# A state-space scan and window attention in one kernel: output products summed by accumulating DMAs from GpSimd's queue

## The chip, the cores and the metric

The kernel runs on one core of one Trainium2 chip. A core has four compute engines with in-order instruction queues of their own: TensorE (PE in the profile; its weight loads are PEld), VectorE (DVE), ScalarE (ACT) and GpSimd (POOL). SyncE (SP) issues DMA transfers, which 16 DMA engines carry out. Engines wait for each other by semaphores. The metric is the device time of one execution in microseconds (us). Before the change it is 7846.2 us, the median of three runs (7838.49 to 7853.48).

## What is computed

The reference applies two layers to x of shape 8 x 192 x 64 x 64 in float32.

Layer 0 widens 192 channels to 384 by a 1x1 product, applies a 3x3 depthwise convolution, and then scans the image in four directions d (rows, columns, and both flipped). Each direction and channel has gates made from a 16-channel proxy. The part that matters here, per direction:

```
hn  = l * x + gl * h_up + gm * h + gr * h_dn      # 8 steps, chunks of 8
out = out * Us + xs * Ds                          # two products for each direction
y   = einsum('bdchw,d->bchw', out_y, w_m)         # the sum over the four directions
y   = grn(layernorm2d(y)); return conv1x1(y, W_out)
```

Layer 1 is window attention with 6 heads on 8x8 windows (layer norm, normalised q and k, only scores at or above the 16th largest kept, softmax, projection) and a feed-forward part with GELU, each with a residual.

## The kernel before

The kernel is one program over 8 images. For each image `front` makes the convolved input and writes it to DRAM in two layouts, `scan` makes the sum y, and `window_row` does layer 1 for 8 rows of 8 windows. Image b is scanned while the windows of image b-1 and the front of image b+1 run. A tile is 128 channels by 512 positions. In `scan`, each of 8 steps t has 12 tiles, four directions times three blocks of 128 channels (`ct`), in the order of `TILES`: directions 0, 2, 1, 3. So an image has 96 tiles, and the program 768.

A tile's work (`tile_of` and `rest`, lines 685 to 816): TensorE makes the gates (L681), ScalarE takes their absolute values (L738, L760), VectorE multiplies gates by the state (L745, L747), GpSimd and VectorE add up the gates' sum and the products (L769, L777, L784, L788), ScalarE makes a reciprocal by Ln and Exp (L780, L782), and VectorE writes the new state (L810). Tiles go in pairs (`PAIRS`). When the second tile of a pair has its state, `outputs` makes four products on TensorE in four of the six PSUM banks, and `onto_sum` (L834) handles each of the two tiles: VectorE writes `dx` (L836) and `hu` (L841), two products of a PSUM bank with the input and with the state. GpSimd then does the sum over directions in the tile `y3` (128 x 3 x 512, two buffers):

- direction 0: `y3 = hu + dx`, one addition (L848);
- direction 2: `dx = dx + hu` (L850), then `y3 = y3 + dx` (L856);
- directions 1 and 3: the same with L850, then L858, where dx is read with a stride of 64 elements, because these directions hold a tile as columns x rows (`by`), while y3 is kept as rows x columns.

`norm` (L864) takes the finished y3: mean over channels on TensorE (L871), spread back (L883), subtract on VectorE (L894), squares on ScalarE (L899), and so on, then SP writes it to DRAM (L931).

The order of instructions on each engine is not the program order. Every call of `plan` makes a `Step` with an engine, a cost in nanoseconds (hold and latency), and what it reads and writes. `Plan.order` runs a list scheduler over all steps with these costs (`vec`, `act`, `gp`, `mg`, `dma`) and with a model of TensorE's clock (`TICK`, `ENTRY`), repeats it `RUNS` times with ranks taken from the last run, keeps the shortest, and then writes the steps down in that order. Dependencies become semaphore waits. So a change of a cost changes the order on all engines, but no instruction's own time. Tiles in SBUF (`Held`) have a tag and a number of buffers; a step that needs a buffer waits for the last user of an earlier one. In `window_row` the transposed q and k (`qkT`, tag `four`, two tiles of two buffers, L1186) are made by TensorE's transposes (L1192), and the feed-forward's hidden tile `hd` (one buffer, L1455) is read by L1496.

Of the kernel before, what the change touches and what calls it, by code (L numbers as in the profile page):

```python
# [26 lines left out]
ALU = mybir.AluOpType  # L27
# [27 lines left out]
class Held:  # L55
# [11 lines left out]
    def __call__(self):  # L67
        return self.tile
# [9 lines left out]
class Plan:  # L78
# [5 lines left out]


    HOP = 35.0
    TICK, ENTRY = 10240 / 3, 3060.0
    RUNS = 12
    SLACK = 40.0

    def __init__(self):
# [1 line left out]
        self.parts = {}  # L93
        self.rank, self.lane = 0.0, 0

    def __call__(self, engine, cost, fn, r=(), w=()):
        s = Step(engine, fn, cost, self.rank, self.lane, len(self.steps))
        self.steps.append(s)
        deps = set()
        for item in r:  # L100
            for k in self._overlaps(item, self.writers):
                deps.update(self.writers[k])
        for item in w:
            for k in self._overlaps(item, self.writers):
                deps.update(self.writers[k])
            for k in self._overlaps(item, self.readers):
                deps.update(self.readers[k])
        for item in list(r) + list(w):
            h = item[0] if isinstance(item, tuple) else item
            if isinstance(h, Held) and s not in h.users:  # L110
                if not h.users:
                    s.makes.append(h)
                else:
                    deps.add(h.users[0])
                h.users.append(s)
                s.held.append(h)
# [12 lines left out]
        deps.discard(s)  # L129
        s.before = len(deps)  # L130
        for d in deps:
            d.after.append(s)
        return s
# [12 lines left out]
    def order(self):  # L146

        before = [s.before for s in self.steps]
        tiles = {h: h.left for s in self.steps for h in s.held}
        best = None
        for _ in range(self.RUNS):
            for s, k in zip(self.steps, before):
                s.before, s.ready = k, 0.0
            for h, k in tiles.items():
                h.left, h.end, h.next = k, 0.0, None  # L160
            run = self.run()
            if best is None or self.length < best[0]:
                best = self.length, run, [s.start for s in run]
            for s in run:
                needs = [d.start for d in s.after] + [h.next.start for h in s.held if h.next]
                s.rank = min(needs, default=s.end) - (s.end - s.start)
        self.length, run, starts = best
        for s, t in zip(run, starts):
            s.start = t
        return run  # L170
# [118 lines left out]
def tile_ss2d_then_window_attention(ctx: ExitStack, tc: tile.TileContext, a: dict, out: bass.AP):  # L289
# [170 lines left out]
    vec = lambda n: (n / 0.96 + 69, 88)  # L460
    act = lambda n, more=50.0: (n / 1.2 + more, 110)
    gp = lambda n: (n * 2.3 + 52, 42)
    mm = lambda slots, n, share=1.0: (65.0, slots * n * 4.16, share)
    tiled = lambda cycles, share=1.0: (150.0, cycles, share)
    split = (275.0, 6475.0, 1.0)
    turned = lambda n, share=1.0: (60.0, 262.0 * n, share)

    mg = lambda share=1.0: (120.0, 2270.0, share)
    dma = lambda n=1, kb=0: (max(350.0 * n, 5.4 * kb), 2600.0)
    tiny = (150.0, 60.0)  # L470
    log_c = {}
    log_half = blank("log_half", [P, 1], math.log(0.5) / 3)
# [143 lines left out]
    def scan(b, xs, xsT, z, made):  # L616
# [68 lines left out]
        def tile_of(t, d, ct, xp, x0, y3, last):  # L685
# [85 lines left out]
            if last:  # L771
                last()

            def rest():
                if t > 0:
                    rr = Held(spool, [P, 512], "rr", bufs=2)
# [20 lines left out]
                        w=[nb],  # L797
                    )
                    plan("POOL", gp(512), lambda: nc.gpsimd.tensor_mul(one(), one(), rr()), r=[rr], w=[(pr, 0)])  # L799
                    plan(  # L800
                        "DVE",
                        vec(512),
                        lambda: nc.vector.scalar_tensor_tensor(nb(), nb(), 2.0, one(), ALU.subtract, ALU.mult),  # L803
                        r=[(pr, 0)],
                        w=[nb],
                    )
                    plan(
                        "DVE",
# [4 lines left out]
                    )  # L813
                waiting.append((d, ct, xd, xv, h_key))
                if len(waiting) == 2:
                    outputs(waiting, nb if t > 0 else None)

            def outputs(pair, nb):

                banks = [[bank("g") for _ in range(2)] for _ in range(2)]  # L820

                at = PAIRS.index(tuple(p[:2] for p in pair)) * P

                def both():
                    for k in range(2):
                        for m in range(2):
                            project(banks[k][m](), w_g2, 64 * k + RG * m, RG, at, xp())

                plan("PE", mg(), both, r=[xp, nb] if nb else [xp], w=banks[0] + banks[1])
                for (d, ct, xd, xv, h_key), (pd, pu) in zip(pair, banks):  # L830
                    onto_sum(d, ct, xd, xv, h_key, pd, pu)
                pair.clear()

            def onto_sum(d, ct, xd, xv, h_key, pd, pu):  # L834
                dx = Held(spool, [P, 512], "dx")
                plan("DVE", vec(512), lambda: nc.vector.tensor_mul(by(dx(), d), by(pd(), d), xv()), r=[pd, xd], w=[dx])  # L836
                hu = Held(spool, [P, 512], "hu")
                plan(
                    "DVE",
                    vec(512),  # L840
                    lambda: nc.vector.tensor_mul(like(hu(), d), like(pu(), d), state(d, ct)),  # L841
                    r=[pu, h_key],
                    w=[hu],
                )
                yt = lambda: y3()[:, ct, :]
                y_key = y3, ct
                if d == 0:
                    plan("POOL", gp(512), lambda: nc.gpsimd.tensor_add(yt(), hu(), dx()), r=[hu, dx], w=[y_key])  # L848
                    return
                plan("POOL", gp(512), lambda: nc.gpsimd.tensor_add(dx(), dx(), hu()), r=[hu], w=[dx])  # L850

                def onto():
                    y = by(yt(), 0)
                    if d == 2:

                        nc.gpsimd.tensor_add(y, y, by(dx(), 0))  # L856
                    else:
                        nc.gpsimd.tensor_add(y, y, dx().rearrange("p (c i) -> p i c", c=CH))  # L858

                plan("POOL", gp(512) if d == 2 else (1540.0, 40.0), onto, r=[dx], w=[y_key])  # L860

            return rest

        def norm(t, y3):  # L864
# [22 lines left out]
            m4 = Held(spool, [P, P], "m4", tag="xq", bufs=1)  # L887
            plan("PE", tiled(1553.0), lambda: means(pm, y3), r=[y3], w=[pm])
            plan("ACT", act(P), lambda: nc.scalar.copy(m4(), pm()[:, 0:P]), r=[pm], w=[m4])
            plan("PE", tiled(2203.0), lambda: spread(pm, m4), r=[m4], w=[pm])  # L890
            plan(
                "DVE",
                vec(1536),
# [26 lines left out]
                r=[pv],  # L920
                w=[sq],
            )
            plan("PE", tiled(2203.0), lambda: spread(pv, rr), r=[sq], w=[pv])
            plan(
                "DVE",
                vec(1536),
# [85 lines left out]
    def window_row(b, g, z, sc, bb):  # L1012
# [170 lines left out]
        plan("DVE", (2373.0, 90.0), unit, r=[nn], w=[qk])  # L1183
        yield
        plan.lane = 8
        qkT = [Held(lpool, [HALF, 2, GT], "four", bufs=2) for _ in range(2)]  # L1186
        for k in range(4):
            pt = bank()

            def turn(k=k, pt=pt):  # L1190
                for tt in range(NT):
                    nc.tensor.transpose(  # L1192
                        pt()[0:HALF, tt * P : (tt + 1) * P], qk()[:, tt, k * HALF : (k + 1) * HALF], ident
                    )

            plan("PE", turned(4), turn, r=[qk], w=[pt, (qkT[k // 2], "room")])
            plan(
                "ACT",
                act(512),
                lambda k=k, pt=pt: nc.scalar.copy(qkT[k // 2]()[:, k % 2, :], pt()[0:HALF, :]),  # L1200
                r=[pt],
                w=[(qkT[k // 2], k % 2)],
            )
            yield

# [8 lines left out]
        def scores():  # L1214
            for w in range(WS):
                tok = slice(w * 64, w * 64 + 64)
                for r in range(3):
                    rows = slice(32 * r, 32 * r + 32)
                    for j in range(2):
                        nc.tensor.matmul(  # L1220
                            pas[r]()[64 * j : 64 * j + 64, tok],
                            lhsT=qkT[0]()[rows, j, tok],
                            rhs=qkT[1]()[rows, j, tok],
                            start=True,
                            stop=True,
                        )

        plan("PE", tiled(2550.0, 0.6), scores, r=qkT, w=pas + [(at, "room")])
        for r in range(3):
            rng = slice(r * WS, (r + 1) * WS)  # L1230
            plan(
# [114 lines left out]
                                stop=True,  # L1346
                            )

        plan("PE", tiled(2350.0, 0.5), attend, r=[at, v], w=po + [("oT", "room")])
        for w in range(2):  # L1350
            plan(
                "ACT",
# [288 lines left out]
```

## Time and profile before

| what | value |
|---|---|
| median of three runs | 7846.2 us |
| profiled execution, its own time | 7831.69 us |
| its span, first to last instruction | 7829.6 us |
| mean granted TensorE clock | 0.849 |
| GpSimd's additions for the sum: L850, L858, L848, L856 | 738.2 + 593.4 + 252.6 + 250.1 us busy, 1344 instructions |
| VectorE's products for the sum: L841, L836 | 517.8 + 388.7 + 130.2 us busy, 1536 instructions |
| DMA moved | 695.53 MB, mean 89 GB/s |

The profile is that of one execution. Busy time is when an engine works on an instruction; idle time before an instruction is put down to what released it last. Instructions that only issue DMAs are not counted as busy. A stage in which an engine is busy 90% of the time may be bound by it; one in which three engines are all near that needs a look at who waits for whom. In a list of waits a row reads: engine and instruction that waited, the instruction that it waited for, total us, times, longest. In a table of stretches a row reads: the stretch in us, its length, busy us and number of instructions of PE, PEld, DVE, ACT and POOL, the granted clock, the DMA engines' busy share and GB/s.

### The profile page before, as it was taken

To read this page: it belongs to the slowest core of one execution; us is meant where nothing else is said; L and a number is where in the kernel's file an instruction comes from. 1 tells how busy PE (TensorE), PEld (TensorE's weight loads), DVE (VectorE), ACT (ScalarE), POOL (GpSimd) and SP (SyncE) were. 2 spreads that over 40 slices of the span, in tenths; PEclk is the share of its full clock that TensorE was granted. 3 is DMA by queue.
4 is the path that set the end of the run, shared out by engine and by line. 5 is a ranking of instruction groups with operands and counts; after the bars stand their busy time and mean duration, and the time that the engine had idled before them with its cause. 6 is when DMAs were issued, how large, how long until landed. Compare 5 with 4: busy or idle time off the path is not lost.

```text
span 7829.6 us, 144584 instructions
## 1 busy us (share of the span) xinstructions
PE 6807.6 (87%) x51224; PEld 3516.3 (45%) x51224; DVE 6279.8 (80%) x15421; ACT 4911.0 (63%) x9657; POOL 6212.0 (79%) x6302
## 2 busy tenths in 40 slices
PE   5788888888999889889998889988888898788888
PEld 2333344444444444444444444444444444344554
DVE  1377778899788978889889888888899989999443
ACT  1355446775666656766677656767566656666665
POOL 0388878899788978888889878888799989899332
PEclk8788779987898878888898779988878878788998
DMA  7666445312543135322553124431211121111110
GB/s 183 181 170 167 125 123 146 100 50 65 151 115 78 47 112 137 87 69 59 140 141 85 44 85 129 115 80 51 58 48 49 50 61 51 46 47 46 25 25 14
DMA packets 1037929, 695.53 MB, mean 89 GB/s; under 512 B 704116, under 2 KB 860215, under 8 KB 1037207
## 3 DMA queue, kind: packets, MB, share of 16 engines
q1 hardware_dynamic: 1035830, 684.99, 33.0%
q8 instruction: 407, 6.67, 0.4%
q14 instruction: 316, 2.58, 0.1%
q10 hardware_dynamic: 1376, 1.30, 0.1%
HBM read 453.43 MB, written 232.67 MB: 88 GB/s over the span
## 4 chain that ended last, share of the span: by engine, by line
DVE 21%; PE 19%; POOL 15%; ACT 8%; issue 4%; DMA 0%; POOLq 0%; SPq 0%; ACTq 0%; DVEq 0%
PE g L681 6%; PE lp L1496 4%; POOL pr L799 3%; POOL ab L769 2%; POOL pr L784 2%; DVE rest L1249 2%; POOL dx L850 2%; PE lp L1105 2%; POOL pr L788 2%; DVE pr L745 2%; DVE nb L803 1%; DVE pr L747 1%; PE lp L1462 1%; POOL y L858 1%; DVE top L1247 1%
## 5 line engine op out<-in xcount | busy, mean ns | idle before, releaser
L681 PE MATMUL g<-xe,w_g 32*128 32x512 f32 x3648 | 1273.0, 768 | 271.1 <-DVE dx L836 106.9
L681 PE MATMUL g<-xo,w_g 32*128 32x512 f32 x3648 | 1156.1, 728 | 218.5 <-DVE dx L836 123.8
L784 POOL TENSOR_TENSOR pr<-pr 128x512 f32<-128x512 f32 x672 | 878.0, 1307 | 192.7 <-DVE pr L745 137.1
L769 POOL TENSOR_TENSOR ab<-ab 128x512 f32<-128x512 f32 x672 | 873.3, 1300 | 162.6 <-ACT ab L738 157.8
L738 ACT ACTIVATE ab<-g 128x512 f32<-128x512 f32 x1344 | 782.2, 596 | 333.3 <-PE nb L681 145.7
L799 POOL TENSOR_TENSOR pr<-pr,rr 128x512 f32<-128x512 f32 x672 | 869.2, 1294 | 125.7 <-ACT rr L782 106.9
L788 POOL TENSOR_TENSOR pr<-pr 128x512 f32<-128x512 f32 x672 | 865.4, 1289 | 17.2
L850 POOL TENSOR_TENSOR dx<-dx,hu 128x512 f32<-128x512 f32 x576 | 738.2, 1290 | 121.8 <-DVE hu L841 108.2
L780 ACT ACTIVATE rr<-nb,eps 128x512 f32<-128x512 f32 x672 | 461.3, 686 | 566.5 <-DVE nb L777 564.4
L681 PEld LDWEIGHTS g<-xe,w_g 32*128 32x128 f32 x3648 | 447.3, 216 | 811.2 <-DVE dx L836 227.8
L568 PE MATMUL lp<-strip,w_cv 128*32 128x256 f32 x9216 | 682.0, 440 | 142.5 <-DMA strip<-pad 123.5
L681 PEld LDWEIGHTS g<-xo,w_g 32*128 32x128 f32 x3648 | 390.9, 206 | 731.5 <-DVE dx L836 250.2
L1496 PE MATMUL lp<-hd,w_f 128*64 128x256 f32 (+1 forms) x2304 | 585.1, 492 | 33.7 <-ACT hd L1482 23.6
L795 DVE SCALAR_TENSOR_TENSOR nb<-nb,rr 128x512 f32<-128x512 f32 x672 | 464.5, 691 | 186.8 <-ACT rr L782 185.9
L858 POOL TENSOR_TENSOR y<-y,dx 128x512 f32<-128x512 f32 x384 | 593.4, 1554 | 2.2
L803 DVE SCALAR_TENSOR_TENSOR nb<-nb,pr 128x512 f32<-128x512 f32 x672 | 464.4, 691 | 152.0 <-POOL pr L799 149.7
L777 DVE TENSOR_TENSOR nb<-nb,ab 128x512 f32<-128x512 f32 x672 | 464.5, 691 | 110.3 <-POOL ab L769 94.2
L568 PEld LDWEIGHTS lp<-strip,w_cv 128*32 128x32 f32 x9216 | 304.5, 123 | 543.0 <-issue 274.3
L848 POOL TENSOR_TENSOR y<-hu,dx 128x512 f32<-128x512 f32 x192 | 252.6, 1320 | 340.6 <-DVE hu L841 337.9
L841 DVE TENSOR_TENSOR hu<-g,hid 128x512 f32<-128x512 f32 x768 | 517.8, 678 | 4.9 <-PE g L681 4.4
L681 PE MATMUL nb<-xe,w_g 32*128 32x512 f32 x672 | 511.9, 852 | 11.1 <-DVE hid L810 8.8
L760 ACT ACTIVATE nb<-nb 128x512 f32<-128x512 f32 x672 | 398.7, 593 | 183.6 <-DVE pr L745 107.7
(203 smaller groups left out, 16680.0 us busy)
## 6 DMA issues: line engine op xcount, KB each, us to landing
strip<-pad SPq DMA_DIRECT2D x1152, 132.0 KB
xd<-xsT SPq DMA_DIRECT2D x384, 256.0 KB
pad<-xin SPq DMA_DIRECT2D x192, 264.0 KB
xs<-st SPq DMA_DIRECT2D x192, 256.0 KB
xsT<-sn SPq DMA_DIRECT2D x192, 256.0 KB
xd<-xs SPq DMA_DIRECT2D x192, 256.0 KB
x<-xs SPq DMA_DIRECT2D x64, 768.0 KB
z<-y SPq DMA_DIRECT2D x64, 768.0 KB
```

Of the source, the lines that this page charges most:

```text
L568: nc.tensor.matmul(pc()[q * RG : (q + 1) * RG, k * 256 : (k + 1) * 256].rearrange("p (h w) -> p h w", h=4), lhsT=w_cv[:, ct, q, dx, :], rh ...
L681: nc.tensor.matmul(dst, lhsT=w[rows, col : col + P], rhs=xp[rows, :], start=True, stop=True)
L738: lambda r=r: nc.scalar.activation(ab()[:, r, :], g[r](), AF.Abs),
L769: plan("POOL", gp(512), lambda: nc.gpsimd.tensor_add(ab()[:, 0, :], ab()[:, 0, :], ab()[:, 1, :]), w=[ab])
L784: plan("POOL", gp(512), lambda: nc.gpsimd.tensor_add(one(), one(), pr()[:, 1, :]), r=[(pr, 1)], w=[(pr, 0)])
L788: lambda: nc.gpsimd.tensor_add(one(), one(), pr()[:, 2, :]),
L799: plan("POOL", gp(512), lambda: nc.gpsimd.tensor_mul(one(), one(), rr()), r=[rr], w=[(pr, 0)])
L803: lambda: nc.vector.scalar_tensor_tensor(nb(), nb(), 2.0, one(), ALU.subtract, ALU.mult),
L841: lambda: nc.vector.tensor_mul(like(hu(), d), like(pu(), d), state(d, ct)),
L850: plan("POOL", gp(512), lambda: nc.gpsimd.tensor_add(dx(), dx(), hu()), r=[hu], w=[dx])
L858: nc.gpsimd.tensor_add(y, y, dx().rearrange("p (c i) -> p i c", c=CH))
L1496: nc.tensor.matmul(dst[:, at : at + rhs.shape[-1]], lhsT=lhsT, rhs=rhs, **flags)
```

## The change

Each pair of tiles now gets two joint tiles `dxu` of 128 x 2 x 512: one for the two products with the input, one for the two with the state. VectorE writes the products there (L863, L873 in the changed kernel), already in y3's order: in directions 1 and 3 with a stride of 8 elements. For direction 0 the product with the input goes straight into y3. GpSimd's additions are gone; in their place GpSimd's queue issues DMAs that add a joint tile onto y3 in SBUF (`accum_op`): eleven for each step t, 704 in all, 640 of 512 KB and 64 of 256 KB (L883, L893). The tile `qkT` becomes one tile of four blocks that shares the single buffer of `hd`; the DMA descriptors' room in SBUF goes from 512 to 2048 bytes. The planner gets a cost for the new DMA (1000 ns hold, 2500 ns latency), other constants for TensorE's clock and shares, 30 repetitions in place of 12, and ranks that are averaged with those of the run before. The output products of a pair no longer read `nb`; they are ordered behind the steps that made the pair's last state factors (`made_w`).

```diff
-    TICK, ENTRY = 10240 / 3, 3060.0
-    RUNS = 12
+    TICK, ENTRY = 10240 / 3, 3200.0
+    RUNS = 30
...
-    def __call__(self, engine, cost, fn, r=(), w=()):
+    def __call__(self, engine, cost, fn, r=(), w=(), behind=()):
...
-        deps = set()
+        deps = set(behind)
...
-                s.rank = min(needs, default=s.end) - (s.end - s.start)
+                rank = min(needs, default=s.end) - (s.end - s.start)
+                s.rank = (s.rank + rank) / 2 if n else rank
...
-    mm = lambda slots, n, share=1.0: (65.0, slots * n * 4.16, share)
+    mm = lambda slots, n, share=0.96: (65.0, slots * n * 4.16, share)
...
-    mg = lambda share=1.0: (120.0, 2270.0, share)
+    mg = lambda share=0.9: (120.0, 2270.0, share)
...
+    accumulate = (1000.0, 2500.0)
...
-                plan("PE", mg(), both, r=[xp, nb] if nb else [xp], w=banks[0] + banks[1])
-                for (d, ct, xd, xv, h_key), (pd, pu) in zip(pair, banks):
-                    onto_sum(d, ct, xd, xv, h_key, pd, pu)
+                plan("PE", mg(), both, r=[xp], w=banks[0] + banks[1], behind=made_w)
+                onto_sum(pair, banks)
...
-            def onto_sum(d, ct, xd, xv, h_key, pd, pu):
...
-                if d == 0:
-                    plan("POOL", gp(512), lambda: nc.gpsimd.tensor_add(yt(), hu(), dx()), r=[hu, dx], w=[y_key])
-                    return
-                plan("POOL", gp(512), lambda: nc.gpsimd.tensor_add(dx(), dx(), hu()), r=[hu], w=[dx])
...
-                plan("POOL", gp(512) if d == 2 else (1540.0, 40.0), onto, r=[dx], w=[y_key])
+            def onto_sum(pair, banks):
+
+                cts = [p[1] for p in pair]
+                lo, step = min(cts), abs(cts[1] - cts[0])
+                parts = Held(spool, [P, 2, 512], "dxu", bufs=3), Held(spool, [P, 2, 512], "dxu", bufs=3)
+
+                def order_y(ap, d):
+
+                    return like(ap, d) if d % 2 == 0 else ap.rearrange("p (i c) -> p c i", c=CH)
+
+                for m, part in enumerate(parts):
+                    todo = []
+                    for (d, ct, xd, xv, h_key), bank2 in zip(pair, banks):
+                        src = bank2[m]
+                        first = m == 0 and d == 0
...
+                                lambda dst=dst, src=src, xv=xv, d=d: nc.vector.tensor_mul(
+                                    order_y(dst(), d) if d % 2 else by(dst(), d), by(src(), d), xv()
+                                ),
...
+                                lambda dst=dst, src=src, d=d, ct=ct: nc.vector.tensor_mul(
+                                    order_y(dst(), d), like(src(), d), state(d, ct)
+                                ),
...
+                    if len(todo) == 2:
+                        plan(
+                            "POOL",
+                            accumulate,
+                            lambda part=part: nc.gpsimd.dma_start(
+                                y3()[:, lo : lo + step + 1 : step, :], part(), accum_op=ALU.add
+                            ),
+                            r=[part],
+                            w=[(y3, ct) for ct in todo],
+                        )
...
-        qkT = [Held(lpool, [HALF, 2, GT], "four", bufs=2) for _ in range(2)]
+        qkT = Held(lpool, [HALF, 4, GT], "four", bufs=1, tag="hd")
...
-    nc = bacc.Bacc("TRN2", target_bir_lowering=False, num_devices=1, dynamic_dma_scratch_size=512)
+    nc = bacc.Bacc("TRN2", target_bir_lowering=False, num_devices=1, dynamic_dma_scratch_size=2048)
```

More of the change, by code (lines that the diff above doesn't have):

```diff
@@ L155, in order @@
         best = None
-        for _ in range(self.RUNS):
+        for n in range(self.RUNS):
             for s, k in zip(self.steps, before):
@@ L462, in tile_ss2d_then_window_attention @@
     gp = lambda n: (n * 2.3 + 52, 42)
-    mm = lambda slots, n, share=1.0: (65.0, slots * n * 4.16, share)
+    mm = lambda slots, n, share=0.96: (65.0, slots * n * 4.16, share)
     tiled = lambda cycles, share=1.0: (150.0, cycles, share)
-    split = (275.0, 6475.0, 1.0)
+    split = (275.0, 6475.0, 0.95)
     turned = lambda n, share=1.0: (60.0, 262.0 * n, share)
-    mg = lambda share=1.0: (120.0, 2270.0, share)
+    mg = lambda share=0.9: (120.0, 2270.0, share)
     dma = lambda n=1, kb=0: (max(350.0 * n, 5.4 * kb), 2600.0)
+    accumulate = (1000.0, 2500.0)
     tiny = (150.0, 60.0)
@@ L772, in tile_of @@
                 last()
+            made_w = []
             def rest():
@@ L799, in rest @@
                     plan("POOL", gp(512), lambda: nc.gpsimd.tensor_mul(one(), one(), rr()), r=[rr], w=[(pr, 0)])
[L800 to L805, printed above, removed]
+                    made_w.append(
+                        plan(
+                            "DVE",
+                            vec(512),
+                            lambda: nc.vector.scalar_tensor_tensor(nb(), nb(), 2.0, one(), ALU.subtract, ALU.mult),
+                            r=[(pr, 0)],
+                            w=[nb],
+                        )
                     )
@@ L815, in rest, with outputs @@
                 if len(waiting) == 2:
-                    outputs(waiting, nb if t > 0 else None)
-            def outputs(pair, nb):
+                    outputs(waiting, made_w)
+            def outputs(pair, made_w):
                 banks = [[bank("g") for _ in range(2)] for _ in range(2)]
@@ L827, in both @@
                             project(banks[k][m](), w_g2, 64 * k + RG * m, RG, at, xp())
-                plan("PE", mg(), both, r=[xp, nb] if nb else [xp], w=banks[0] + banks[1])
-                for (d, ct, xd, xv, h_key), (pd, pu) in zip(pair, banks):
-                    onto_sum(d, ct, xd, xv, h_key, pd, pu)
+                plan("PE", mg(), both, r=[xp], w=banks[0] + banks[1], behind=made_w)
+                onto_sum(pair, banks)
                 pair.clear()
-            def onto_sum(d, ct, xd, xv, h_key, pd, pu):
[L835 to L846, printed above, removed]
-                if d == 0:
-                    plan("POOL", gp(512), lambda: nc.gpsimd.tensor_add(yt(), hu(), dx()), r=[hu, dx], w=[y_key])
-                    return
[L850 to L858, printed above, removed]
-                plan("POOL", gp(512) if d == 2 else (1540.0, 40.0), onto, r=[dx], w=[y_key])
@@ new lines, in onto_sum @@
+            def onto_sum(pair, banks):
[9 more added lines that the diff above has]
+                        first = m == 0 and d == 0
+                        if first:
+                            dst = lambda ct=ct: y3()[:, ct, :]
+                        else:
+                            dst = lambda part=part, ct=ct: part()[:, int(ct > lo), :]
+                            todo.append(ct)
+                        if m == 0:
+                            plan(
+                                "DVE",
+                                vec(512),
+                                lambda dst=dst, src=src, xv=xv, d=d: nc.vector.tensor_mul(
+                                    order_y(dst(), d) if d % 2 else by(dst(), d), by(src(), d), xv()
+                                ),
+                                r=[src, xd],
+                                w=[(y3, ct) if first else (part, ct)],
+                            )
+                        else:
+                            plan(
+                                "DVE",
+                                vec(512),
+                                lambda dst=dst, src=src, d=d, ct=ct: nc.vector.tensor_mul(
+                                    order_y(dst(), d), like(src(), d), state(d, ct)
+                                ),
+                                r=[src, h_key],
+                                w=[(part, ct)],
+                            )
+                    if len(todo) == 2:
+                        plan(
+                            "POOL",
[5 more added lines that the diff above has]
+                            w=[(y3, ct) for ct in todo],
+                        )
+                    elif todo:
+                        plan(
+                            "POOL",
+                            accumulate,
+                            lambda part=part, ct=todo[0]: nc.gpsimd.dma_start(
+                                y3()[:, ct, :], part()[:, int(ct > lo), :], accum_op=ALU.add
+                            ),
+                            r=[part],
+                            w=[(y3, todo[0])],
+                        )
@@ L889, in norm @@
             plan("ACT", act(P), lambda: nc.scalar.copy(m4(), pm()[:, 0:P]), r=[pm], w=[m4])
-            plan("PE", tiled(2203.0), lambda: spread(pm, m4), r=[m4], w=[pm])
+            plan("PE", tiled(2203.0, 0.93), lambda: spread(pm, m4), r=[m4], w=[pm])
             plan(
@@ L922, in norm @@
             )
-            plan("PE", tiled(2203.0), lambda: spread(pv, rr), r=[sq], w=[pv])
+            plan("PE", tiled(2203.0, 0.93), lambda: spread(pv, rr), r=[sq], w=[pv])
             plan(
@@ L1194, in turn @@
                     )
-            plan("PE", turned(4), turn, r=[qk], w=[pt, (qkT[k // 2], "room")])
+            plan("PE", turned(4), turn, r=[qk], w=[pt, (qkT, "room")])
             plan(
@@ L1199, in window_row @@
                 act(512),
-                lambda k=k, pt=pt: nc.scalar.copy(qkT[k // 2]()[:, k % 2, :], pt()[0:HALF, :]),
+                lambda k=k, pt=pt: nc.scalar.copy(qkT()[:, k, :], pt()[0:HALF, :]),
                 r=[pt],
-                w=[(qkT[k // 2], k % 2)],
+                w=[(qkT, k)],
             )
@@ L1221, in scores @@
                             pas[r]()[64 * j : 64 * j + 64, tok],
-                            lhsT=qkT[0]()[rows, j, tok],
-                            rhs=qkT[1]()[rows, j, tok],
+                            lhsT=qkT()[rows, j, tok],
+                            rhs=qkT()[rows, 2 + j, tok],
                             start=True,
@@ L1226, in scores @@
                         )
-        plan("PE", tiled(2550.0, 0.6), scores, r=qkT, w=pas + [(at, "room")])
+        plan("PE", tiled(2550.0, 0.6), scores, r=[qkT], w=pas + [(at, "room")])
         for r in range(3):
@@ L1347, in attend @@
                             )
-        plan("PE", tiled(2350.0, 0.5), attend, r=[at, v], w=po + [("oT", "room")])
+        plan("PE", tiled(2350.0, 0.65), attend, r=[at, v], w=po + [("oT", "room")])
         for w in range(2):
```

## The prediction

> **What bounds the kernel now.** First the busy shares of the page, then the table of stretches: the start until the first output products (0 to 290 us), the eight scans (290 to 7290), the last image's windows (7290 to 7829), and two stretches without a front stage.
>
> ```profile
> PE 6807.6 (87%) x51224; PEld 3516.3 (45%) x51224; DVE 6279.8 (80%) x15421; ACT 4911.0 (63%) x9657; POOL 6212.0 (79%) x6302
> 0.00:290.00 290.00, 176.33 (x1457) 79.25 (x1458) 28.59 (x69) 60.46 (x85) 2.29 (x8) 0.80 0.73 188
> 290.00:7290.00 7000.00, 6181.81 (x45749) 3154.64 (x45748) 6014.45 (x14175) 4511.16 (x8866) 6056.22 (x5968) 0.85 0.34 90
> 7290.00:7829.00 539.00, 449.45 (x4022) 282.46 (x4018) 236.74 (x1180) 339.41 (x707) 153.49 (x328) 0.90 0.09 20
> 5700.00:6100.00 400.00, 351.19 (x2298) 185.43 (x2295) 371.64 (x922) 275.68 (x551) 369.28 (x376) 0.83 0.18 51
> 6500.00:6900.00 400.00, 329.99 (x2399) 175.41 (x2400) 366.12 (x850) 260.32 (x517) 369.40 (x364) 0.84 0.17 48
> ```
>
> All that the change touches lies in the 7000 us. There PE is busy 88.3%, POOL 86.5%, DVE 85.9%. PE's figure contains its slow clock (0.85): at full clock the same work is about 6182 x 0.85 = 5255 us, 75%. So PE is not the bound; DVE and POOL are, level with each other. Neither is full, because each waits for the other and for PE and ACT. The list of waits shows it, with PE held by DVE, which empties PSUM:
>
> ```profile
> PEld g L681 <- DVE dx L836: 478.0, 343, 8.3
> DVE nb L795 <- ACT rr L782: 185.9, 159, 4.4
> DVE nb L803 <- POOL pr L799: 149.7, 162, 4.2
> POOL pr L784 <- DVE pr L745: 137.1, 86, 5.1
> PE lp L568 <- DMA strip<-pad: 123.5, 41, 8.1
> ```
>
> The price of GpSimd's additions, and of strided access, is in the groups, kept apart by shape:
>
> ```profile
> L850 POOL TENSOR_TENSOR dx<-dx,hu 128x512 f32<-128x512 f32 x576 | 738.2, 1290 | 121.8 <-DVE hu L841 108.2 <-DVE dx L836 11.6 <-ACT ab L738 0.2
> L858 POOL TENSOR_TENSOR y<-y,dx 128x512 f32<-128x512 f32 x384 | 593.4, 1554 | 2.2
> L848 POOL TENSOR_TENSOR y<-hu,dx 128x512 f32<-128x512 f32 x192 | 252.6, 1320 | 340.6 <-DVE hu L841 337.9 <-DVE dx L836 2.1
> L856 POOL TENSOR_TENSOR y<-y,dx 128x512 f32<-128x512 f32 x192 | 250.1, 1306 | 1.6
> L582 ACT ACTIVATE st<-lp,vecs 128x512 f32<-128x512 f32 x192 | 222.9, 1161 | 179.0 <-PE lp L568 158.3 <-DMA xsT<-sn 7.4 <-ACT xin L533 5.3
> L595 ACT ACTIVATE sn<-lp,vecs 128x512 f32<-128x512 f32 x192 | 128.6, 670 | 1.2 <-DMA xsT<-sn 1.2
> ```
>
> L858 differs from L856 only in reading dx with a stride: +248 ns. L582 writes what L595 writes, with a stride of 64 elements: +491 ns, twice the time.
>
> **What the Trainium skill says.** "DMA: Bandwidth & Descriptors", section "SWDGE vs HWDGE vs iDMA": a DMA that accumulates must come from GpSimd, whose cores compute its descriptors, so GpSimd stays occupied for each. The same page, "Rules for kernel authors": an accumulating DMA reads its destination and writes it later, so another one onto the same bytes must wait for the first one's semaphore. No such DMA is in this trace. "SBUF — State Buffer", section "A bandwidth-pool intuition that's wrong (but worth ruling out)", gives lines of 16 bytes and a penalty for each access that crosses into a new one. The ACT and POOL rows above agree with it. "VectorE: DVE Perf Modes", section "Mode 1×", says of VectorE's one-result-per-cycle mode that "fp32, weird strides, PSUM operands" all work, and counts unused port width alone as its cost. No strided VectorE write is in this trace, so nothing here decides between the two pages.
>
> **The change, part by part.**
>
> Removed: the four groups of additions, 738.2 + 593.4 + 252.6 + 250.1 = 1834 us of POOL, all in the 7000 us. POOL's work there falls from 6056 to 4222 us.
>
> Added on POOL: 704 DMA issues. The page on DMA puts GpSimd's start of a DMA at about 1 us (section "Specifications"); SP's issues of xd (L697) in this trace take 0.33 us. I bound the hold at 0.6 to 1.5 us and take 1.0: 704 us, so 4926.
>
> Added as a wait: in the changed order of instructions, 640 of the 704 wait for an earlier DMA of the same sum, and POOL is in order, so the gate additions behind (L769, L784, L788, L799 of before) wait too, and DVE's L777 and L803 for those. Pricing the POOL instructions that stand between two such DMAs by their rows of before, the gap is under 0.65 us in 57 cases and under 3.5 us in 301. Landing: the page's fit ("Anatomy of one DMA — SWDGE (gpsimd) path") is 2.0 + bytes / 436e3 us, 3.2 us for 512 KB; the destination is also read, and SP's transfers use the same 16 engines. As an estimate I take 3.5 us after the issue, between 2.5 and 6. The sum of (landing - gap) over the cases below it is 281 us at 2.5, 561 at 3.5, 1052 at 5, 1404 at 6. So POOL is taken for 4926 + 561 = 5487 us, 78% of 7000; between 4222 + 422 + 281 = 4925 and 4222 + 1056 + 1404 = 6682.
>
> DVE: the count of products is the same, 1536. In directions 1 and 3, 768 of them now write with a stride of 32 bytes. Below: 0. Above: one more cycle for each of 512 elements, 533 ns (ACT's twofold time carried over), 768 x 0.533 = 409 us. In the likeliest case I take 0, since DVE's element takes 1.04 ns against 0.83 of ACT, and keep the other for the range. A second new wait on DVE is for a free `dxu`: three buffers, two for each pair. A pair comes every 7000 / 384 = 18.2 us; one part is held some 1.4 + 1.0 + 3.5 = 6 us, the other 4.5 us longer, about 16 of 3 x 18.2 buffer-us, so waits should be few; at a landing of 6 us it is some 24.
>
> DMA engines: 352 MB more, 808 us of all engines if each byte passes once, 1616 if twice. The share 0.34 becomes 0.46 to 0.57. The cover is the rest; the price, if transfers stretch by a fifth, is about 25 us on PE's 123.5 us for strips and a fifth of SP's landings, which loads ahead.
>
> Edits at nothing: the shared buffer of `qkT` and `hd` makes L1192 wait for both halves of L1496, where before it could run between them. In the scans other PE work covers that; in the last 539 us it would cost at most 8 rows x 3.4 us (the second half's 2.8 + 0.6) = 27 us. The mean over channels on PE now waits for the last landings of a step, and everything behind it on PE too: 64 x 3.5 = 224 us if it came straight behind, nothing if the order leaves the planned 2.5 us; 64 us for one us too little. It is counted within the utilisation below. `behind` instead of `nb` drops a wait on DVE's last read at most. The new order as such has no price from a row; it is in the spread.
>
> The sum for the likeliest case: DVE remains, with 6014 us to do. Where POOL and DVE were level it was busy 85.9%; the best stretch shows 92.9% (371.64 of 400). With POOL at 78% and new DMA waits I take the middle, 89.4%: 6014 / 0.894 = 6727 us in place of 7000, a gain of 273. The span becomes 7829.6 - 273 = 7557. The profiled execution's own time is 2.1 us above its span and the median 14.5 us above that: 7574 us. PE would then need 5255 / 6727 = 78% of full-clock time, which needs a clock near 0.88 at 89% busy; before 0.85.
>
> **Rivals.**
>
> Better: DVE runs at 92.9% throughout, since nothing level with it is left: 6014 / 0.929 = 6474, -526, about 7320 us. For it: the best stretches have POOL at 92% too, so DVE without it could go there. Against: those lack the front stage, and ACT's and PE's waits remain.
>
> Slower, by VectorE's strided writes: 409 us more work, 6423 / 0.894 = 7185, +185, about 8032 us. Break-even is (7000 x 0.894 - 6014) / 768 = 0.32 us more for each write. For it: ACT's and POOL's rows. Against: POOL's 248 ns would still leave a gain.
>
> POOL's blocked queue takes the place of the additions: hold and stalls together reach 1834 us at a hold of 1.0 when the landing is 5.2 us. At 5.5 us (1228 us of stalls) POOL has 6154 us, +98; at its present 86.5% that is +113, about 7960. For it: 344 of 640 gaps are under 5 us. Against: part of these stalls falls into time in which POOL waits anyway.
>
> PE is what holds: it is busy 88.3%, and its clock sinks when it is fed badly; if its rate can't rise, the time stays at about 7840. Against: 0.90 with 90% busy occurs elsewhere (the last stretch has 0.90).
>
> **How the numbers follow.** Likeliest case 0.42 (its own range 7450 to 7700), better 0.13, strided writes 0.25, blocked queue 0.13, PE 0.07. About 0.2% is what a measurement of this kernel can tell from no change. Faster: 0.42 + 0.13, of the strided case 0.03 (below break-even), of PE's 0.02, together 0.60. Same: 0.05, mostly of PE's case. Slower: 0.35. The range: of the better case 0.08 lies below 7340, of the slower two 0.12 above 7980.
>
> **What would show it.** Right: POOL's additions gone and its busy time near 4400 us plus issues; DVE's products with strides at 0.68 us; DVE busy near 89% of a shorter middle; POOL waits for DMA y below 560 us; PE clock 0.87 or more. Wrong: strided L863 and L873 at 1.0 us or more; POOL idle before the DMA issues or the gate additions behind over 1100 us; DVE waiting for `dxu` by hundreds of us; strip waits of PE several times 123.5 us.

## The result, and the profile after

| | median of runs | ratio to before (95% interval) |
|---|---|---|
| before | 7842.34 us | |
| changed | 8419.15 us (8413.55 to 8438.81) | 1.0741 (1.0715 to 1.0767) |

The changed kernel is 7.4% slower; 7574 us was forecast, with 7980 as the upper end of the range. A word on terms: the hold of a DMA is the time that its issue keeps GpSimd busy, and its landing is the time from the issue until the data have arrived and whoever waits for them is released. First the busy shares of the page after the change:

```profile
PE 7082.6 (84%) x51224; PEld 3609.1 (43%) x51224; DVE 6503.9 (77%) x15421; ACT 4902.9 (58%) x9657; POOL 5138.6 (61%) x5662
```

Then its table of stretches, divided as before into the start, the scans and the last windows (busy us of PE, PEld, DVE, ACT and POOL, granted clock, DMA share and GB/s):

```profile
0.00:290.00 290.00, 172.39 (x1461) 77.85 (x1462) 30.09 (x72) 60.48 (x85) 1.75 (x7) 0.82 0.74 189
290.00:7880.00 7590.00, 6455.83 (x45740) 3249.95 (x45739) 6231.60 (x14142) 4499.31 (x8855) 4979.11 (x5321) 0.83 0.58 129
7880.00:8412.00 532.00, 454.35 (x4026) 281.30 (x4025) 242.26 (x1209) 343.17 (x719) 157.69 (x335) 0.92 0.10 21
```

The loss lies in the scans, which take 7590 us in place of 7000; the start and the end are as before. GpSimd lost over 1000 us of work there (its DMA issues, 692 us, are counted as busy here), and yet the kernel is slower. VectorE has 217 us more to do, 6231.60 us where it was 6014.45, but it is busy only 82.1% of the stretch, where it was 85.9%. So of the 590 us, 217 are added work of VectorE, and 373 are added idle time. The list of waits of the changed kernel says for what (lines from it: engine and line, what it waited for, total us, times, longest):

```profile
POOL y L883 <- DMA y<-dxu: 555.1, 169, 9.2
POOL y L883 <- DVE dxu L863: 284.7, 156, 5.6
POOL y L883 <- DVE dxu L873: 103.3, 42, 8.0
DVE nb L808 <- POOL pr L803: 345.8, 208, 7.5
DVE nb L781 <- POOL ab L771: 231.1, 119, 13.0
DVE dxu L873 <- DMA y<-dxu: 84.3, 20, 7.5
PE lp L909 <- DMA y<-dxu: 100.2, 34, 10.2
POOL y L893 <- DMA y<-dxu: 29.4, 4, 10.8
PE lp L570 <- DMA strip<-pad: 116.6, 44, 8.2
```

One of VectorE's two waits for gate additions in the kernel before stands in the prediction; this is the other, in the kernel before:

```profile
DVE nb L777 <- POOL ab L769: 94.2, 110, 3.7
```

GpSimd stands before an accumulating DMA until the one before it has landed. Behind it stand the gate additions, and VectorE's two waits for these (L777 and L803 before, L781 and L808 now) grew from 94.2 + 149.7 to 231.1 + 345.8 us, by 333 us. The groups by shape give the prices of the issues and the products (busy us, mean ns, idle time before them):

```profile
L883 POOL DMA_DIRECT2D y<-dxu x640 | 635.1, 994 | 1750.8 <-DMA y<-dxu 555.1 <-DMA strip<-pad 293.0 <-DVE dxu L863 284.7
L873 DVE TENSOR_TENSOR dxu<-g,hid 128x512 f32<-128x512 f32 x768 | 678.9, 886 | 84.3 <-DMA y<-dxu 84.3
L863 DVE TENSOR_TENSOR dxu<-g,xd 128x512 f32<-128x512 f32 x576 | 547.6, 951 | 40.2 <-DMA y<-dxu 23.2 <-PE g L683 17.0
L863 DVE TENSOR_TENSOR y<-g,x 128x512 f32<-128x512 f32 x192 | 130.4, 679 | 12.0 <-PE g L683 11.8
```

The page's row of GpSimd's DMA queue (packets, MB, share of 16 engines' span):

```profile
q0 software_dynamic: 125952, 352.37, 23.3%
```

And its row of their issues (KB each, median us from issue to landing):

```profile
y<-dxu POOLq DMA_DIRECT2D x640, 512.0 KB, 5.3
```

An issue holds GpSimd for 0.99 us, as assumed. Its landing takes 5.3 us, not 3.5. The writes into `dxu` are longer than those into y3 (L863, 679 ns); half of L873 and two thirds of L863's `dxu` group are strided.

### The profile page after: what moved, and what is told of

It is laid out like the page before. It is cut to its first block, busy times and chain, and to the rows that moved or that the text cites. A ratio compares the mean times of both kernels' runs of the same rounds, so it can differ in the third digit from the quotient of the medians.

```text
span 8412.0 us, 145405 instructions
## 1 busy us (share of the span) xinstructions
PE 7082.6 (84%) x51224; PEld 3609.1 (43%) x51224; DVE 6503.9 (77%) x15421; ACT 4902.9 (58%) x9657; POOL 5138.6 (61%) x5662
## 3 DMA queue, kind: packets, MB, share of 16 engines
q0 software_dynamic: 125952, 352.37, 23.3%
## 4 chain that ended last, share of the span: by engine, by line
DVE 18%; PE 15%; POOL 8%; DMA 7%; ACT 6%; issue 5%; SPq 0%; POOLq 0%; DVEq 0%; ACTq 0%
DMA y<-dxu 7%; PE g L683 3%; PE lp L1534 3%; POOL pr L803 2%; DVE dxu L863 2%; POOL pr L792 2%; PE lp L1500 2%; DVE rest L1287 1%; POOL pr L788 1%; DVE dxu L873 1%; DVE pr L749 1%; DVE pr L747 1%; DVE nb L808 1%; DVE hid L816 1%; PE lp L1143 1%
## 5 line engine op out<-in xcount | busy, mean ns | idle before, releaser
L883 POOL DMA_DIRECT2D y<-dxu x640 | 635.1, 994 | 1750.8 <-DMA y<-dxu 555.1
L683 PE MATMUL g<-xo,w_g 32*128 32x512 f32 x3648 | 1283.9, 746 | 368.4 <-DVE dxu L863 151.7
L788 POOL TENSOR_TENSOR pr<-pr 128x512 f32<-128x512 f32 x672 | 933.5, 1389 | 292.2 <-DVE pr L747 190.5
L771 POOL TENSOR_TENSOR ab<-ab 128x512 f32<-128x512 f32 x672 | 933.1, 1389 | 151.1 <-ACT ab L740 144.7
L803 POOL TENSOR_TENSOR pr<-pr,rr 128x512 f32<-128x512 f32 x672 | 899.4, 1338 | 178.6 <-ACT rr L786 148.2
L792 POOL TENSOR_TENSOR pr<-pr 128x512 f32<-128x512 f32 x672 | 914.0, 1360 | 30.5
L683 PEld LDWEIGHTS g<-xo,w_g 32*128 32x128 f32 x3648 | 434.2, 212 | 947.4 <-DVE dxu L863 264.9
L570 PE MATMUL lp<-strip,w_cv 128*32 128x256 f32 x9216 | 691.8, 444 | 134.4 <-DMA strip<-pad 116.6
L873 DVE TENSOR_TENSOR dxu<-g,hid 128x512 f32<-128x512 f32 x768 | 678.9, 886 | 84.3 <-DMA y<-dxu 84.3
L808 DVE SCALAR_TENSOR_TENSOR nb<-nb,pr 128x512 f32<-128x512 f32 x672 | 469.4, 699 | 348.3 <-POOL pr L803 345.8
L781 DVE TENSOR_TENSOR nb<-nb,ab 128x512 f32<-128x512 f32 x672 | 466.0, 693 | 246.3 <-POOL ab L771 231.1
L863 DVE TENSOR_TENSOR dxu<-g,xd 128x512 f32<-128x512 f32 x576 | 547.6, 951 | 40.2 <-DMA y<-dxu 23.2
L683 PE MATMUL nb<-xo,w_g 32*128 32x512 f32 x672 | 477.1, 797 | 9.8 <-DVE hid L816 9.8
L683 PE MATMUL nb<-xe,w_g 32*128 32x512 f32 x672 | 475.4, 793 | 1.7 <-DVE hid L816 1.6
```

What stands on the lines that cost most here:

```text
L570: nc.tensor.matmul(pc()[q * RG : (q + 1) * RG, k * 256 : (k + 1) * 256].rearrange("p (h w) -> p h w", h=4), lhsT=w_cv[:, ct, q, dx, :], rh ...
L683: nc.tensor.matmul(dst, lhsT=w[rows, col : col + P], rhs=xp[rows, :], start=True, stop=True)
L771: plan("POOL", gp(512), lambda: nc.gpsimd.tensor_add(ab()[:, 0, :], ab()[:, 0, :], ab()[:, 1, :]), w=[ab])
L788: plan("POOL", gp(512), lambda: nc.gpsimd.tensor_add(one(), one(), pr()[:, 1, :]), r=[(pr, 1)], w=[(pr, 0)])
L792: lambda: nc.gpsimd.tensor_add(one(), one(), pr()[:, 2, :]),
L863: lambda dst=dst, src=src, xv=xv, d=d: nc.vector.tensor_mul(order_y(dst(), d) if d % 2 else by(dst(), d), by(src(), d), xv()),
```

## Experiments

Two suspects were left from the rivals, each just over its break-even: VectorE's strided writes, and GpSimd's queue blocked until a landing. A third was the new order itself. All kernels are the changed one with the edit shown, except where said. The excerpts show the DMA for two tiles (L883); where it changes, the one for a single tile (L893) changes in the same way.

**Writes without a stride.**

```diff
-                    return like(ap, d) if d % 2 == 0 else ap.rearrange("p (i c) -> p c i", c=CH)
+                    return like(ap, d)
```

> The changed kernel with the products of directions 1 and 3 written without a stride (the re-ordering to rows x columns is left out, so the sum mixes positions); order and DMAs unchanged. Theory S (VectorE's strided writes cost the time): L863 and L873 all at 0.68 us, 768 x 0.41 = 315 us less VectorE work, about 8050 us. Theory Q (GpSimd's queue, blocked until each accumulating DMA has landed, costs the time): little moves, 8300 to 8420 us, and GpSimd's idle time before L883 stays at about 1700 us.

Measured: 8309.56 us, 1.0595 (1.0565 to 1.0626) of before; 110 us less than the changed kernel, inside the range given for the blocked queue; GpSimd's wait for landings before L883 stays, at 558.2 us. The group of this run:

```profile
L873 DVE TENSOR_TENSOR dxu<-g,hid 128x512 f32<-128x512 f32 x768 | 523.1, 683 | 95.3 <-DMA y<-dxu 95.1
```

683 ns where the mix took 886, so a strided write takes 2 x 886 - 683 = 1089 ns: 406 ns more, 768 x 0.406 = 312 us of VectorE's time. Only a third of that is seen in the end; VectorE has idle time in the blocked kernel that can take up the rest. The stride alone doesn't explain the loss.

**No accumulating DMAs**, with strides, and without both. The planned step stays in its place in the order and does nothing:

```diff
-                            lambda part=part: nc.gpsimd.dma_start(
-                                y3()[:, lo : lo + step + 1 : step, :], part(), accum_op=ALU.add
-                            ),
+                            lambda: None,
```

> The changed kernel in the same order with the accumulating DMAs not issued (only direction 0's input product is in the sum); strided writes stay. Theory Q: GpSimd has no issue and no wait for y, 7750 to 7900 us. Theory S: 8250 us or more.

Measured: 7709.75 us, 0.9831 (0.9798 to 0.9863), 40 us below the range given for the blocked queue and far from that of the strides.

> Both at once: no strided writes and no accumulating DMAs (the sum is left incomplete and not re-ordered). It is the likeliest case of the prediction with no price for the DMAs. If Q and S are all there is, about 7450 to 7550 us; if the new order of instructions itself costs time, 7700 us or more.

Measured: 7491.08 us, 0.9552 (0.9522 to 0.9581). The scans of the two runs, the first with strides and the second without, each up to 540 us before its end:

```profile
290.00:7175.20 6885.20, 6201.69 (x45558) 3139.56 (x45555) 6175.80 (x14097) 4485.11 (x8828) 4305.11 (x4605) 0.86 0.35 91
```

```profile
290.00:6943.40 6653.40, 6012.50 (x45567) 3078.65 (x45564) 5922.82 (x14103) 4474.16 (x8827) 4304.00 (x4605) 0.87 0.36 95
```

VectorE is busy 5922.82 / 6653.40 = 89.0%, and 6175.80 / 6885.20 = 89.7% with the strides. Here its work is close to the bound: 253 us more of it lengthen the scans by 232 us, and the whole program by 219. PE is as busy (90.4% and 90.1%, at clocks of 0.87 and 0.86), so VectorE isn't alone. The DMAs, all in all, cost 8419 - 7710 = 709 us beside the strides, and 8310 - 7491 = 818 us without them: the two costs overlap, and what each is worth depends on which goes first.

**The planner alone**, on the kernel before: its constants, repetitions and averaged ranks.

> The kernel before with the changed planner alone (constants, shares, 30 repetitions, averaged ranks); additions on GpSimd as before. Theories Q and S: the planner is not at fault, 7700 to 7880 us. Theory P (the new order costs the time): 8100 us or more.

Measured: 7796.37 us, 0.9948 (0.9925 to 0.997). The new planner is worth half a per cent by itself. That the changed kernel's own order isn't at fault either, as long as there is no landing to wait for, is seen in the run with neither DMAs nor strides, which keeps it.

**Where in the DMAs.** Three runs take one part each away. In the first the DMA goes onto one of eight zeroed DRAM tiles in turn, so that none waits for the one before:

```diff
-                                y3()[:, lo : lo + step + 1 : step, :], part(), accum_op=ALU.add
+                                away(), part(), accum_op=ALU.add
```

> The changed kernel with each accumulating DMA sent onto one of eight zeroed tiles in DRAM in turn, not onto y3 (the sum is left incomplete); same order, same number of issues and source bytes, strided writes stay. No DMA waits for the one before it. Theory W (the wait for the earlier DMA's landing, at the head of GpSimd's queue, is what the DMAs cost): 7720 to 7900 us, near the run without DMAs. Theory H (the issue's hold of 0.9 us, the traffic and the dxu buffers cost it): 8150 us or more.

Measured: 7875.6 us, 1.0046 (1.003 to 1.0062). The landing is later still, 6.5 us, but no DMA stands in line for it. VectorE's waits for GpSimd in this run, then its wait for a free `dxu` and PE's for strips, and the row of GpSimd's DMA queue:

```profile
DVE nb L818 <- POOL pr L813: 103.5, 120, 2.5
DVE nb L791 <- POOL ab L781: 40.2, 49, 4.1
DVE dxu L883 <- DMA away<-dxu: 39.9, 16, 4.4
PE lp L580 <- DMA strip<-pad: 151.5, 54, 7.9
```

```profile
q0 software_dynamic: 101376, 352.37, 27.5%
```

VectorE waits 144 us for gate additions where it waits 577 in the changed kernel, 433 us less. The traffic isn't what was saved: the same bytes take a larger share of the DMA engines here. So 543 of the 709 us belong to waits for landings (and to the destination, which is DRAM here). That is GpSimd's wait, 584.5 us in all, but not it alone: PE's 100.2 us for y before the mean over channels (L909) and part of VectorE's 107.5 us for `dxu` went with it. No run takes these apart, though the 433 us of VectorE's waits for gate additions speak for GpSimd's queue as the larger part.

In the second the DMA keeps its place and its waits, but moves 8 elements of each row:

```diff
-                                y3()[:, lo : lo + step + 1 : step, :], part(), accum_op=ALU.add
+                                y3()[:, lo : lo + step + 1 : step, 0:8], part()[:, :, 0:8], accum_op=ALU.add
```

> The changed kernel with each accumulating DMA moving 8 elements of a row's 512 (the rest is left out of the sum); same order, same issues, same waits. Theory W: the landing falls to about 2.5 us, the planned value, GpSimd's idle time before L883 falls by half or more, 7750 to 7950 us. Theory H: the hold stays, 8200 us or more.

Measured: 7988.54 us, 1.0192 (1.0138 to 1.0245), a little above the range expected. What the trace answers on all of y's DMAs, of the changed kernel first and of this run second:

```profile
DMA to landing us min/median/max: 3.3/5.4/11.4
DMA to landing us min/median/max: 2.4/2.9/9.2
```

And GpSimd's wait for them that is left in this run's list:

```profile
POOL y L883 <- DMA y<-dxu: 149.0, 67, 5.6
```

A landing of 2.9 us in place of 5.4 takes 431 us off, though an issue of so many small rows holds GpSimd longer (1233 ns). So the waiting is in the main a matter of the landing's length; the transfers are all but gone as well, but in the run before they stayed and the loss did not.

In the third a GpSimd copy of half the joint tile stands where the issue stood:

```diff
-                            lambda part=part: nc.gpsimd.dma_start(
-                                y3()[:, lo : lo + step + 1 : step, :], part(), accum_op=ALU.add
-                            ),
+                            lambda part=part: nc.gpsimd.tensor_scalar(held, part()[:, 0, :], 1.0, 0.0, ALU.mult, ALU.add),
```

> The changed kernel with each accumulating DMA replaced by a GpSimd copy of half the joint tile into a private tile (nothing more is added to the sum): it waits for VectorE's products and holds GpSimd for about as long as an issue, but there is no transfer and no landing. Order and strided writes stay. If the 166 us between the run without DMAs (7710 us) and the one with DMAs sent away (7876 us) come from the hold and from waiting in line for the products: 7800 to 7900 us. If they come from the transfers: 7700 to 7760 us.

Measured: 7735.71 us, 0.9871 (0.9851 to 0.989), 26 us above the run without DMAs. It falls on the second side. The group of the copies, 640 of the 704, and PE's wait for strips in this run:

```profile
L884 POOL TENSOR_SCALAR held<-dxu 128x512 f32<-128x512 f32 x640 | 407.6, 637 | 575.5 <-DMA xs<-st 279.2 <-DVE dxu L864 209.0 <-DVE dxu L874 82.8
PE lp L571 <- DMA strip<-pad: 103.3, 35, 8.0
```

The copies take 447.6 us of GpSimd's time in all, and these and the line-up behind VectorE's products are nearly free. That leaves 140 us, up to the run with DMAs sent away, for what else the two differ in: a hold longer by some 0.28 us, the transfers (PE's wait for strips is 48 us longer with them), and `dxu` held until they land (39.9 us of waits). How much is due to each is not settled.

**A planner that knows the landing and the stride's price.**

```diff
-    accumulate = (1000.0, 2500.0)
+    accumulate = (900.0, 4500.0)
...
-                                vec(512),
+                                vec(512) if d % 2 == 0 else (1010.0, 88.0),
```

> The changed kernel, with the planner told what was measured: an accumulating DMA holds 900 ns and lands 4500 ns later, a strided VectorE write takes 1010 ns (and its loop ends at a ranking that it can't complete). All of its work is kept. Theory O (the order was made for a landing of 2.5 us, and that is why queues stall): 7750 to 7950 us. If an in-order queue can't be arranged around eleven chained landings in each step: 8150 us or more.

Measured: 8165.51 us, 1.0417 (1.0387 to 1.0448): 254 us better than the changed kernel, and just on the far side of the line drawn. GpSimd still waits 378.2 us for a landing before L886, the same DMA there. A part of the loss is an order made with wrong costs, for landings and strided writes together, as one run changed both; the larger part stays with eleven chained landings in each step.

**Plain copies in place of accumulating ones.**

```diff
-                                y3()[:, lo : lo + step + 1 : step, :], part(), accum_op=ALU.add
+                                y3()[:, lo : lo + step + 1 : step, :], part()
```

> The changed kernel with plain copies from GpSimd's queue in place of the accumulating ones (the sum holds only the last part written); same order, bytes, waits and strided writes. If reading the destination is what makes the landing 5.3 us and not the 3.2 us of the fit: landing 3.3 to 4.2 us, 8050 to 8250 us. If any transfer of this size and queue lands so late here: landing 5 us or more, 8350 to 8450 us.

Measured: 8029.98 us, 1.0239 (1.0209 to 1.0269), 20 us below the range given for a landing that is shorter. The row of GpSimd's DMA queue in this run:

```profile
q0 software_dynamic: 97280, 352.37, 11.9%
```

The group of the issues:

```profile
L883 POOL DMA_DIRECT2D y<-dxu x640 | 409.5, 640 | 1407.9 <-DVE dxu L863 302.4 <-DMA strip<-pad 290.8 <-DMA y<-dxu 279.9
```

And the page's row of their landing:

```profile
y<-dxu POOLq DMA_DIRECT2D x640, 512.0 KB, 3.8
```

The same bytes take 11.9% of 8024 us as plain copies and 23.3% of 8412 us as accumulating ones: 955 against 1960 us of all 16 engines. Accumulating doubles the transfer, lengthens the landing from 3.8 to 5.3 us and the issue from 640 to 994 ns, and costs 389 us in all.

**A version with fewer of them.** If the price is landings in a chain and VectorE's strides, GpSimd should keep the addition of dx and hu, write it with the stride itself, and issue one DMA for each pair: five in each step in place of eleven, far apart. All the work is kept. The planner is told 900 and 4500 ns, and `dxu` has two buffers in place of three.

```diff
+                        dst = lambda ct=ct: part()[:, int(ct > lo), :].rearrange("p (i c) -> p c i", c=CH)
...
+                        lambda dst=dst, hu=hu, dx=dx, d=d: nc.gpsimd.tensor_add(dst(), like(hu(), d), like(dx(), d)),
...
+                        lambda: nc.gpsimd.dma_start(y3()[:, lo : lo + step + 1 : step, :], part(), accum_op=ALU.add),
```

> A version that keeps all the work: GpSimd adds dx and hu of each tile as before (writing directions 1 and 3 with a stride), VectorE writes without a stride, and one accumulating DMA for each pair adds onto y3, 320 in place of 704, planned with 900 and 4500 ns. GpSimd: 1834 - 843 us of additions + 0.25 x 384 + 320 x 0.9 = about 5750 us busy in place of 6212. If stride and blocked queue are all there is against such DMAs: 7600 to 7740 us, faster than before. If the DMAs cost time in another way: 7840 us or more.

Measured: 7654.95 us, 0.9766 (0.9738 to 0.9794).

> The version with one accumulating DMA for each pair once more, unchanged, for a firmer ratio: between 0.973 and 0.980 of the kernel before if the first result holds.

Measured: 7645.28 us, 0.9755 (0.9739 to 0.9771), faster than before, than the changed kernel and than the new planner alone. Busy shares of the first of these two runs:

```profile
PE 6770.8 (89%) x51224; PEld 3493.2 (46%) x51224; DVE 6259.6 (82%) x15421; ACT 4891.6 (64%) x9657; POOL 5688.2 (74%) x6046
```

And its groups of GpSimd's additions and issues:

```profile
L873 POOL TENSOR_TENSOR dxu<-hu,dx 128x512 f32<-128x512 f32 x576 | 745.5, 1306 | 114.1 <-DVE hu L857 112.1
L873 POOL TENSOR_TENSOR y<-hu,dx 128x512 f32<-128x512 f32 x192 | 247.3, 1295 | 355.6 <-DVE hu L857 355.3
L881 POOL DMA_DIRECT2D y<-dxu x256 | 251.0, 980 | 45.4 <-DMA y<-dxu 25.6 <-POOL dxu L873 17.2 <-POOL nn L1205 0.5
```

The landing takes as long as in the changed kernel (5.3 us by the page), but GpSimd waits 25.6 us for it in all. The version differs in several things at once, so it shows that the additions can be moved at a gain, not what each of its edits is worth.

The steps from the kernel before to the changed one, each a difference of two medians. The split holds for this order of steps only; with the DMAs in place the strides cost 110 us, not 219.

| step | us |
|---|---|
| before, in the first set of experiments | 7839 |
| new planner on the kernel before | -43 |
| additions off GpSimd and the other edits of the change, no DMAs, no strides | -305 |
| VectorE's strided writes | +219 |
| GpSimd held and in line for the products | +26 |
| DMAs, sent away | +140 |
| waiting for landings, onto y3 in place of DRAM | +543 |
| changed | 8419 |

## Why the prediction was wrong

- **What bounds the kernel, and the gain.** Right in the main. With both costs absent VectorE is busy 89.0% of the scans, against the 89.4% taken, and the granted clock is 0.87, near the 0.88 asked for; PE is just as busy, which the forecast expected too. The time is then 348 us below the kernel before, 305 of them beside the planner's share, where 273 was forecast with the DMAs at work. The gain is there; two costs eat it.
- **The strided writes taken at 0.** The first step that failed. The rival had put the break-even at 0.32 us more for each write and named ACT's and GpSimd's rows for it; measured is 0.41. I took 0 because VectorE's element takes longer. The term measures 312 us of work, and 219 us of time without the DMAs, 110 with them. The page "SBUF — State Buffer" of the Trainium skill (section "Specifications (TRN2)") gives 16-byte lines and a penalty at each crossing into a new one; VectorE's 406 ns agree with it, while GpSimd's writes with the same stride show next to nothing of it (1306 ns with two thirds of them strided, against 1295). "VectorE: DVE Perf Modes" (section "Mode 1×") says that strides work in that mode, not that they are free; it gave no ground for a cost of 0.
- **The landing of 3.5 us.** The second. It is 5.3 us, inside the bound of 2.5 to 6. A plain copy lands after 3.8 us, 0.6 us above the estimate of 3.2 us from the fit in "DMA: Bandwidth & Descriptors" (section "Anatomy of one DMA — SWDGE (gpsimd) path"). Accumulating adds 1.5 us; the forecast had added 0.3 us to the fit for it and for the traffic together.
- **The stalls taken as absorbed by GpSimd's slack.** The step that made the miss so large. I added stalls to GpSimd's work, found 78%, and let VectorE's use rise. Their amount was met, and by luck: 561 us forecast, 555.1 + 29.4 = 584.5 us measured. At a landing of 5.3 us the forecast's own sum gives about 1160 us, so the gaps between the DMAs must have been longer than priced (GpSimd also waits 388 us for VectorE's products before L883, which is a likely reason). What failed is what a stall costs. GpSimd's share of busy time was not what counted: it is 61% now. A wait at the head of its queue keeps back the gate additions behind it, and VectorE waits for these. Taking all waits for landings away, PE's and VectorE's included, gave 543 us. The hold, which the planner knew, is nearly free (26 us for 447.6 us of copies). So "part of these stalls falls into time in which POOL waits anyway", the argument against the rival, fell. The rival made the same sum and was short too: its +113 us at 5.5 us and the +185 us of the strided rival make 298 us together, and 577 were measured. That the planner had been told 2.5 us, and nothing of the strides, is part of the loss: 254 us.
- **The edits taken at nothing.** The last stretch takes 532 us, against 539, so no cost of the shared buffer of `qkT` and `hd` is seen there. PE waits 100.2 us for y before L909, within the 0 to 224 given, but this was no part of the sum by itself. `dxu` keeps VectorE waiting 84.3 + 23.2 us, which is more than "few". The DMA engines' extra time is 1960 us, above the 808 to 1616 given, and their share 0.58, just above 0.46 to 0.57; PE's wait for strips, 116.6 us, shows no price for it.
- **The signs to look for.** Of the four signs of being wrong two came true: strided writes over 1.0 us, and GpSimd idle before the DMA issues for over 1100 us (1750.8, of which 287 stand before the first of them). Of the signs of being right only GpSimd's busy time came true (5138.6 us, 4447 without the issues); its waits for y, 584.5 us, are a little over the 560 named, and the granted clock in the scans is 0.83 where 0.87 was asked for.

## What to carry to other kernels

In this kernel a DMA that had to wait for the landing of another blocked whatever stood behind it on the issuing engine; so price such a wait by what is behind it and who waits for that, not by the engine's share of busy time. The accumulating DMAs paid where landings on the same bytes were far apart, so try adding up on an engine first and sending few. And before data are re-ordered in a write, measure the stride on the engine that is the bound: here it was nearly free on another.

## What the runs showed of the hardware

- VectorE's product of PSUM and SBUF, 128 x 512 float32, takes 683 ns when it writes in a row and 1089 ns with a stride of 32 bytes (worked out from a group of which half is strided).
- GpSimd's addition of two such tiles takes 1306 ns on the mean when two thirds of them write with that stride, against 1295 ns for those of the same run in a row. So this stride in its writes is all but free, while a read with a stride of 256 bytes had cost 248 ns.
- The accumulating DMAs within SBUF (640 of 512 KB, 64 of 256 KB) last 1960 / 704 = 2.8 us on all 16 engines on the mean, and 1.4 us as plain copies. Those of 512 KB land 5.3 us after their issue, against 3.8, with the kernel's other transfers beside them.
- Such an issue of 512 KB holds GpSimd for 994 ns on the mean when it accumulates and for 640 ns as a plain copy.
